# Layer 0 of a two-layer image block: TensorE's strip in eight runs of one tile shape, paired 64-column matmuls, two-bank PSUM buffers and a pinned VectorE order

## The chip, the cores and the metric

The kernel runs on one core of one Trainium2 chip. The metric is the device time in microseconds (us) of one execution; the time before is the median of three runs. One more execution was taken by the hardware profiler, and every row of the profile comes from that one.

## What is computed

`x` is (4, 64, 256, 256) in float32. Two layers run one after the other, each on a group-normalised input, and each adds its result to `x`. The change touches layer 0 alone:

```
x  = x + L0(group_norm(x))          # layer 0, changed
x  = x + L1(group_norm(x))          # layer 1, two state-space blocks and a fusion, unchanged

L0: h = w_in x                      # 64 -> 3*170 channels
    gate, x_sp, x_fr = split(h)
    sp = depthwise 3x3 conv(x_sp)
    fr = irfft2(rfft2(x_fr in 8x8 patches) * fft_weight)
    out = w_out (gelu(gate) * (sp + fr))   # 170 -> 64 channels
```

## The kernel before

Layer 0 cuts each of the four images (batches) into 32 strips of 8 rows, so 128 strips in all. The 170 channels are worked on as 64 + 64 channels ("a") and 42 channels ("b"), which take different ways.

For the 128 "a" channels the 3x3 convolution is done on TensorE. `products` (L726) forms it from sums and differences of neighbouring input columns: `v14` (difference, by GpSimd, L657) and `v23` (sum and difference, by VectorE, L659 and L660), into two PSUM tiles `m14` and `m23`, in a "third" part whose contraction is 64 rows deep (tile shape 64\*128) and a full part (128\*128). A strip has two halves of its columns, so each of these comes twice. ScalarE copies a part of `m23` out (L748) and VectorE makes the two outer combinations `y` from it (L750, L751).

For the spectral branch, `spec1` (L676) transposes patches and multiplies by `w_in` (64\*128, three groups of tiles per strip, copied out by ScalarE into `hs`, L689), `spec2` (L691) transforms (64\*64, three groups, scaled out by VectorE into `hw`, L702). `inverse_a` (L753) adds the inverse transform of the "a" channels onto `m14` (64 columns wide, shape 128\*64), and `inverse_b` (L778) does that for the 42 "b" channels into a PSUM tile `fr` (shape 128\*42).

The "b" channels' convolution is nine multiply-adds on VectorE (`tap_b`, L797 to L806) on `xat` and its row-swapped copy `xen`, made by `inputs_b` (L707, with a DMA at L724) one strip ahead. `gate_a` and `gate_b` (L767, L790) make the gates, ScalarE applies the Gelu, VectorE multiplies. `project` (L812) makes the output for a half strip, VectorE adds the residual (L827) and takes statistics for layer 1 (L830), and a DMA writes the strip to `x1d` (L836).

In one turn of the strip loop three strips are in work: `cur`, the one ahead of it (`nxt`, whose inputs are loaded and transformed) and the one behind it (`prev`, which is gated and projected). TensorE runs in exactly the written order: `mm` (L195) keeps every matmul in program order, so the list of calls at the end of the loop is its order. VectorE, ScalarE, GpSimd and SP (which issues all DMAs) are put in order by the scheduler. The input statistics of the next batch (`stat_add`, L167 to L169, two VectorE instructions a strip) are written at the head of the turn and are free to move; they wait for the loads of `sx` (L161). At the last strip of a batch the next batch's normalisation is worked out from them (`group_norm`, L135 to L152), and the first `spec1` of that batch needs it.

[...] `m14` and `m23` take two each, `fr` one, `po` (projection) one, and all other uses (`spec1`, `spec2`, both gates, `inputs_b`) share a single two-bank buffer named "two". Of the tiles in SBUF, `at` and `er` have three buffers, `pr`, `pn`, `xat`, `xen`, `v14`, `v23` two, `hs`, `acc`, `fub`, `geb` one.

Of the kernel before, what the change touches and what calls it, by code (L numbers as in the profile page):

```python
# [16 lines left out]
C = 64  # L17
# [91 lines left out]
def tile_kernel(ctx: ExitStack, tc: tile.TileContext, x, cst, w0, winp, wdwp, w1, out):  # L109
# [74 lines left out]
    with ExitStack() as l0:  # L184
# [433 lines left out]
        pp = l0.enter_context(tc.tile_pool(name="ps0", bufs=1, space=PSUM))  # L618
        wk = l0.enter_context(tc.tile_pool(name="wk0", bufs=2))

        fr = new(pp, [P, 4, 128], "fr")
        nc.vector.memset(fr, 0.0)
# [3 lines left out]
        def load(b, s, nm, rs):  # L626
# [25 lines left out]
            if s == NS0 - 1:  # L652
# [6 lines left out]
            nc.vector.tensor_tensor(v23[:, :, 0], d1, d2, ALU.add)  # L659
            nc.vector.tensor_tensor(v23[:, :, 1], d2, d1, ALU.subtract)  # L660
# [6 lines left out]
                "v14": v14.rearrange("p r (c k) -> p r k c", k=2), "v23": v23,  # L667
                "hs": new(wk, [P, 2, 4, 2, HID], "hs", 1), "hw": new(wk, [P, 2, 8, HID], "hw"),
            }

# [20 lines left out]
        def spec2(t, i):  # L691
            u0, u1 = UNITS[i]
            n = (u1 - u0) * HID
            ps = new(pp, [P, 2, 512], "two")
            for k in range(2):
                for w in range(2):
                    p = slice(w * C, (w + 1) * C)
                    mm(
                        ps[k * C : (k + 1) * C, w, :n], lhsT=con("qf")[p],
                        rhs=t["hs"][p, k].rearrange("p a h c -> p (a h c)")[:, u0 * HID : u1 * HID], start=True, stop=True,  # L700
                    )
            nc.vector.tensor_tensor(  # L702
                t["hw"][:, :, u0:u1], ps[:, :, :n].rearrange("p w (u c) -> p w u c", c=HID),
                wsp.unsqueeze(1).unsqueeze(1).to_broadcast([P, 2, u1 - u0, HID]), ALU.mult,
            )

        def inputs_b(t):  # L707

            b, s = t["b"], t["s"]
            if s == 0:  # L710
                ps = new(pp, [P, 2, 512], "two").rearrange("p q (r c) -> p (q r) c", c=S)
                mm(ps[:, 0], lhsT=xb, rhs=t["at"][:, 0, 1 : S + 1], start=True, stop=True)
                nc.scalar.copy(t["xat"][:, 0, 1 : S + 1], ps[:, 0])
            else:
                nc.scalar.copy(t["xat"][:, 0], last_at[b][:, 4])
            ps = new(pp, [P, 2, 512], "two").rearrange("p q (r c) -> p (q r) c", c=S)
            for i in range(2):
                mm(
                    ps[:, 2 * i : 2 * i + 2], lhsT=xb, rhs=t["at"][:, 1 + 2 * i : 3 + 2 * i, 1 : S + 1], start=True, stop=True
                )  # L720
            nc.scalar.copy(t["xat"][:, 1:5, 1 : S + 1], ps)
            last_at[b] = t["xat"]
            for k in range(2):
                nc.sync.dma_start(out=t["xen"][k * C : (k + 1) * C], in_=t["xat"][(1 - k) * C : (2 - k) * C, k : k + 4])  # L724

        def products(t, half, name, third):  # L726
# [3 lines left out]
            if third:  # L730
                t[name] = new(pp, [P, 2, 2, 4, 64], name)
# [14 lines left out]
            ps = t.pop("m23").rearrange("p e k m c -> p e k (m c)")  # L746
            m3 = new(wk, [P, 2, 256], "m3")
            nc.scalar.copy(m3, ps[:, :, 1])  # L748
            t["y"] = new(wk, [P, 2, 2, 256], "y", 2)
            nc.vector.tensor_tensor(t["y"][:, :, 0], ps[:, :, 0], m3, ALU.add)  # L750
            nc.vector.tensor_tensor(t["y"][:, :, 1], ps[:, :, 0], m3, ALU.subtract)  # L751

        def inverse_a(t, half):  # L753
            ps = t.pop("m14")
            for j in range(8):
                for e in range(2):
                    for g in range(2):
                        c = slice(g * C, (g + 1) * C)
                        mm(
                            ps[c, e, :, :, j * 8 : (j + 1) * 8], lhsT=t["hw"][:, j // 4, 2 * (j % 4) + half, c],  # L760
                            rhs=con("qj")[:, e * C : (e + 1) * C].rearrange("p (k m c) -> p k m c", k=2, m=4),
                            start=False, stop=(j == 7),
                        )
            y = t["y", half] = t.pop("y").rearrange("p e k x -> p (e k x)")
            nc.vector.tensor_tensor(y, ps.rearrange("p e k m c -> p (e k m c)"), y, ALU.add)  # L765

        def gate_a(t, half):  # L767
# [5 lines left out]
            ge, fu = new(wk, [P, 1024], "ge"), new(wk, [P, 2, 512], "fu", 3)  # L773
            nc.scalar.activation(ge, pg.rearrange("p e x -> p (e x)"), AF.Gelu)
            nc.vector.tensor_tensor(fu.rearrange("p e x -> p (e x)"), t.pop(("y", half)), ge, ALU.mult)
            t["fu", half] = fu

        def inverse_b(t, half):  # L778
            n = HID - 128
            for j in range(8):  # L780
                for o in range(2):
                    mm(
                        fr[o * C : o * C + n, :, j * 16 : (j + 1) * 16], lhsT=t["hw"][:, j // 4, 2 * (j % 4) + half, 128:HID],
                        rhs=con("qi2")[:, o * C : (o + 1) * C].rearrange("p (m c) -> p m c", m=4),
                        start=True, stop=True,
                    )
            o = t["acc"][:, :, half * 128 : (half + 1) * 128]
            nc.vector.tensor_tensor(o, fr, o, ALU.add)

        def gate_b(t):  # L790
            ps = new(pp, [P, 2, 512], "two").rearrange("p q (r c) -> p (q r) c", c=S)
            for i in range(2):
                mm(ps[:, 2 * i : 2 * i + 2], lhsT=gw[:, 2, :], rhs=t["en"][:, 2 * i : 2 * i + 2, :], start=True, stop=True)
            t["geb"] = new(wk, [P, 4, S], "geb", 1)
            nc.scalar.activation(t["geb"], ps, AF.Gelu)

        def tap_b(t, k):  # L797
            dy, dx = k // 3, k % 3
            src = (t["xat"][:, 0:4], t["xen"], t["xat"][:, 1:5])[dy]
            if k == 0:  # L800
                t["acc"] = new(wk, [P, 4, S], "acc", 1)
                nc.vector.tensor_scalar(t["acc"], src[:, :, dx : dx + S], taps[:, 0:1], None, ALU.mult)
                return
            nc.vector.scalar_tensor_tensor(  # L804
# [3 lines left out]
        def fuse_b(t):  # L808
            t["fub"] = new(wk, [P, 4, S], "fub", 1)
            nc.vector.tensor_tensor(t["fub"], t["acc"], t["geb"], ALU.mult)  # L810

        def project(t, half):  # L812
            po = new(pp, [P, 2, 4, 64], "po")
            h = slice(half * 64, (half + 1) * 64)

            def split(v):
                return v.rearrange("p m (c k) -> p k m c", k=2)[:, :, :, h]

            mm(po, lhsT=ow[:, 2, :], rhs=split(t["fub"]), start=True, stop=False)
            fu = t.pop(("fu", half))  # L820
            for e in range(2):
                mm(
                    po[e * C : (e + 1) * C].rearrange("p k m c -> p (k m c)"), lhsT=oa, rhs=fu[:, e], start=False, stop=True
                )
            if half == 0:
                t["x1"] = new(wk, [P, 4, S], "x1")
            nc.vector.tensor_tensor(split(t["x1"]), po, split(t["er"]), ALU.add)  # L827
            c0 = half * 128
            o = t["x1"][:, :, c0 : c0 + 128]
            nc.vector.bn_stats(t["stats2"][:, 2 * t["s"] + half, :], o)  # L830
            if half == 1:
                if t["s"] == NS0 - 1:
                    moments(moments2[t["b"]], t["stats2"])
                r0 = t["s"] * R0
                for k in range(2):
                    nc.sync.dma_start(  # L836
                        out=x1d[t["b"]][:, r0 + k : r0 + R0 : 2, :], in_=t["x1"][k * C : (k + 1) * C]
                    )
# [11 lines left out]
        inputs_b(cur)  # L850
        prev = None
        nxt_stats = None
        for b in range(nb):
            for s in range(NS0):
                if b + 1 < nb:
                    if s == 0:
                        nxt_stats = new(wk, [P, 2 * NS0, 6], "stats1")
                    stat_add(stat_load(ld, b + 1, s), s, nxt_stats)
                if s + 1 < NS0:
                    nxt = load(b, s + 1, *norm)  # L860
                elif b + 1 < nb:
                    norm = norm_of(nxt_stats)
                    nxt = load(b + 1, 0, *norm)
                else:
                    nxt = None

# [8 lines left out]
                def filter_b(*ks):  # L875
                    for k in ks:
                        tap_b(cur, k)

                products(cur, 0, "m23", True)
                behind(gate_a, 1)  # L880
                filter_b(0)
                products(cur, 0, "m23", False)
                ahead(spec1, 0)
                products(cur, 0, "m14", True)
                filter_b(1)
                products(cur, 0, "m14", False)
                ahead(spec1, 1)
                filter_b(2)
                inverse_a(cur, 0)
                inverse_b(cur, 0)  # L890
                ahead(spec2, 0)
                behind(project, 0)
                filter_b(3)
                ahead(inputs_b)
                products(cur, 1, "m23", True)
                products(cur, 1, "m23", False)
                gate_a(cur, 0)
                products(cur, 1, "m14", True)
                filter_b(4)
                ahead(spec2, 1)  # L900
                products(cur, 1, "m14", False)
                filter_b(5)
                gate_b(cur)
                inverse_a(cur, 1)
                filter_b(6)
                ahead(spec1, 2)
                inverse_b(cur, 1)
                ahead(spec2, 2)
                filter_b(7)
                behind(project, 1)  # L910
                filter_b(8)
# [3 lines left out]
        for half in range(2):  # L915
            project(prev, half)
# [575 lines left out]
```

## Time and profile before

| what | value |
|---|---|
| median of three runs (9519.37 to 9529.17) | 9528.11 us |
| the profiled execution, its own time | 9531.23 us |
| its span, first to last instruction | 9529.5 us |
| mean granted TensorE clock | 0.984 |
| layer 0's strips: first TensorE record to last write of x1d issued | 168 to 4696 us |
| a strip, start to start (median of all) | 34.20 us |
| the three strips at the edge between two batches | 43.6, 44.2 and 43.6 us |
| the last strip | 27.4 us |

A start of a strip is taken here where its `gate_b` starts on TensorE, which happens once a strip. The page gives each engine's busy time, and its rows name an instruction by line, engine, operation and tiles (out<-in). For TensorE a row gives the tile shape first (64\*128: 64 rows by 128 columns of the array) and then the sizes. PE is the matmul stream, PEld the weight loads, which can run beside it; L197 is the helper `mm`, so for TensorE one goes by the tiles' names. Since matmuls are pipelined, a record's duration reaches over the start of the next one: the pace is read from start to start. On VectorE, too, an instruction starts some 0.08 us before the one ahead of it ends, unless it needs its result. Idle time is given with what ended it; "issue" means that the profile shows no wait.

### The profile page before, as it was taken

Reading aid. Unit: us, or ns where it says so; the run is one execution under the profiler, and the core shown is the slowest. Engines: PE = TensorE matmul, PEld = TensorE weight load, DVE = VectorE, ACT = ScalarE, POOL = GpSimd, SP = SyncE. Lnnn points to the kernel's source line nnn. Section 1 sums busy time; section 2 is a strip of 40 time slices with the busy share of each in tenths; the row PEclk is TensorE's granted clock in tenths of the full one; section 3 lists DMA queues with packets and bytes.
Section 4 is the critical chain, followed back from the end, with each engine's and each line's share of the span. In section 5 each row is a group of like instructions: output and inputs, shape, how many; then the busy total and the mean of one; then the engine's idle time right before and its main releaser. Section 6 shows DMA issues by size and latency. Waiting matters only on the chain. (4 is left out here: it accounts for less than half of the span.)

```text
span 9529.5 us, 179824 instructions
## 1 busy us (share of the span) xinstructions
PE 9001.7 (94%) x76918; PEld 5698.1 (60%) x76918; DVE 7028.1 (74%) x8960; ACT 2803.2 (29%) x4570; POOL 3348.5 (35%) x2177
## 2 busy tenths in 40 slices
PE   3889999999999999999999999999999999999999
PEld 2555555555555555555565666656666566665666
DVE  6888777777777778777667776777667767667676
ACT  2222222222222222222362222622226222272222
POOL 4111122111121122111265444654436544375443
PEclk9999999999999999999999999999999999999999
DMA  7664333333333333333361333613336233362332
GB/s 172 151 151 103 82 78 82 82 82 81 81 81 81 81 79 84 81 81 81 87 203 50 79 89 91 192 64 89 85 84 194 74 85 83 84 195 74 84 81 71
DMA packets 655565, 938.21 MB, mean 98 GB/s; under 512 B 43184, under 2 KB 584880, under 8 KB 619184
## 3 DMA queue, kind: packets, MB, share of 16 engines
q1 hardware_dynamic: 654768, 926.71, 37.6%
q8 instruction: 606, 9.93, 0.4%
q14 instruction: 191, 1.56, 0.1%
HBM read 583.86 MB, written 275.05 MB: 90 GB/s over the span
## 5 line engine op out<-in xcount | busy, mean ns | idle before, releaser
L197 PE MATMUL m<-v,sw 64*128 64x256 f32 (+1 forms) x8192 | 1601.1, 398 | 0.0
L197 PEld LDWEIGHTS m<-v,sw 64*128 64x128 f32 (+1 forms) x8192 | 1106.4, 189 | 701.2 <-issue 570.8
L1307 POOL TENSOR_TENSOR xr<-xr,fx 128x512 f32<-128x512 f32 x512 | 651.5, 1272 | 1860.7 <-ACT xr L1306 1370.3
L1204 PE MATMUL pst<-fx,wb 64*128 64x256 f32 (+1 forms) x4992 | 1015.8, 437 | 37.4 <-DVE stm L1210 18.3
L765 DVE TENSOR_TENSOR y<-m,y 128x1024 f32<-128x1024 f32 x256 | 313.0, 1223 | 704.5 <-PE m L197 704.5
L804 DVE SCALAR_TENSOR_TENSOR acc<-xat,taps,acc 128x1024 f32<-128x1024 f32 x640 | 819.5, 1281 | 8.2
L1337 POOL TENSOR_TENSOR rs<-ve,mhalf 128x32 f32<-128x32 f32 x128 | 695.5, 5433 | 99.3 <-DVE ve L1210 99.3
L1204 PEld LDWEIGHTS pst<-fx,wb 64*128 64x128 f32 (+1 forms) x4992 | 508.1, 186 | 370.9 <-issue 244.3
L646 POOL MEMSET at<- 128x10 f32 x128 | 14.4, 113 | 1970.6 <-DMA at<-in_x_dram 1700.1
L1210 DVE SCALAR_TENSOR_TENSOR stm<-stm,step,pst 128x512 f32<-128x512 f32 x640 | 478.5, 748 | 232.8 <-PE pst L1204 219.3
L1308 ACT ACTIVATE sq<-xr 128x512 f32<-128x512 f32 x512 | 322.8, 630 | 875.3 <-POOL xr L1307 875.3
L1204 PE MATMUL px<-wb,xr 128*128 128x128 f32 x4096 | 575.0, 284 | 0.0
L197 PEld LDWEIGHTS m<-ct,hw 128*64 128x64 f32 x16384 | 498.5, 138 | 122.0 <-issue 122.0
L1210 DVE SCALAR_TENSOR_TENSOR sto<-sto,step,pst 128x512 f32<-128x512 f32 x512 | 382.8, 748 | 242.5 <-PE pst L1204 231.3
L1204 PEld LDWEIGHTS px<-wb,xr 128*128 128x128 f32 x4096 | 524.9, 194 | 54.2 <-issue 41.8
L689 ACT COPY hs<-two 128x1020 f32<-128x1020 f32 (+1 forms) x384 | 352.1, 917 | 692.6 <-PE two L197 692.6
L197 PE MATMUL m<-ct,hw 128*64 128x64 f32 x16384 | 533.9, 224 | 0.0
L1204 PE MATMUL ph<-sto,wb 128*64 128x128 f32 (+1 forms) x5120 | 528.0, 299 | 0.0
L1204 PE MATMUL ph<-stm,wb 128*64 128x128 f32 (+1 forms) x5120 | 525.0, 299 | 0.0
L1210 DVE TENSOR_TENSOR y<-px,rs 128x512 f32<-128x512 f32 x512 | 354.0, 691 | 231.7 <-PE px L1204 222.7
L1204 PEld LDWEIGHTS ph<-stm,wb 128*64 128x64 f32 (+1 forms) x5120 | 408.9, 147 | 144.6 <-issue 128.1
L804 DVE SCALAR_TENSOR_TENSOR acc<-xen,taps,acc 128x1024 f32<-128x1024 f32 x384 | 492.2, 1282 | 4.2
(319 smaller groups left out, 16636.8 us busy)
## 6 DMA issues: line engine op xcount, KB each, us to landing
strip<-x1d SPq DMA_DIRECT2D x512, 256.0 KB, 7.3
fx<-fxd SPq DMA_DIRECT2D x128, 1024.0 KB, 6.9
at<-in_x_dram SPq DMA_DIRECT2D x248, 320.0 KB, 5.5
xen<-xat SPq DMA_DIRECT2D x256, 258.0 KB, 4.8
sx<-in_x_dram SPq DMA_DIRECT2D x256, 256.0 KB, 4.6
pr<-in_x_dram SPq DMA_DIRECT2D x256, 256.0 KB, 4.1
er<-in_x_dram SPq DMA_DIRECT2D x256, 256.0 KB, 4.7
x1d<-x SPq DMA_DIRECT2D x256, 256.0 KB, 3.4
```

What stands on the lines that cost most here:

```text
L197: tc.keep_in_program_order(nc.tensor.matmul(*args, **kw))
L646: nc.gpsimd.memset(at[:, :, 0 : S + 2 : S + 1], 0.0)
L689: nc.scalar.copy(hs.rearrange("p k h c -> p h k c"), ps[:, :, : n * HID].rearrange("p h (k c) -> p h k c", k=n))
L765: nc.vector.tensor_tensor(y, ps.rearrange("p e k m c -> p (e k m c)"), y, ALU.add)
L804: nc.vector.scalar_tensor_tensor(t["acc"], src[:, :, dx : dx + S], taps[:, k : k + 1], t["acc"], ALU.mult, ALU.add)
L1204: tc.keep_in_program_order(nc.tensor.matmul(*args, **kw))
L1210: return lambda *args, **kw: tc.keep_in_program_order(getattr(nc.vector, name)(*args, **kw))
L1307: nc.gpsimd.tensor_tensor(xr, xr, fx, ALU.add)
L1308: nc.scalar.activation(sq, xr, AF.Square)
L1337: nc.gpsimd.tensor_tensor(r, ve.rearrange("p n c -> p (n c)"), mhalf, ALU.pow)
```

## The change

The same work is put in another order, in other PSUM buffers.

- TensorE's list is written anew so that calls of one tile shape stand together: the third parts of `m23` and `m14` with two `spec1` and `gate_a`; the full parts; `inverse_b` for the whole strip with `project` for the whole strip and `inverse_a`; two `spec2`; and the same for the second half with `gate_b`, `inputs_b` and the last `spec2`.
- `inputs_b`, `gate_b` and the "b" part of `project`, which were matmuls with 128-column weights, become pairs with 64-column weights.
- `inverse_b` takes 64 columns of `hw` in place of 42; `hw` is now one of two fixed tiles with 32 spare columns.
- `fr` and `po` lose their own PSUM banks; "two" has two buffers of two banks, and `fr` and `po` are taken from it.
- Every VectorE instruction of layer 0's strips keeps its program order (`InOrder`). `products`, `inverse_a`, `gate_a` and `project` are cut so that their VectorE parts (`middle`, `outer`, `fuse_a`, `add_b`, `residual`, `finish`) have places of their own; `sums_in` (the two `v23` instructions) moves to the end of the turn before; the input statistics are given two places in the turn (`count`).

```diff
-        pp = l0.enter_context(tc.tile_pool(name="ps0", bufs=1, space=PSUM))
+        pp = l0.enter_context(tc.tile_pool(name="ps0", bufs=2, space=PSUM))
...
-        fr = new(pp, [P, 4, 128], "fr")
-        nc.vector.memset(fr, 0.0)
+        class InOrder:
+            def __getattr__(self, name):
+                return lambda *args, **kw: tc.keep_in_program_order(getattr(nc.vector, name)(*args, **kw))
+        vec = InOrder()
+        hws = [new(wk, [P, 2 * 8 * HID + 32], f"hw{k}", 1) for k in range(2)]
...
+        def sums_in(t, k):
+            d1, d2 = t["d"]
+            vec.tensor_tensor(t["v23"][:, :, k], d2, d1, ALU.subtract if k else ALU.add)
...
             for i in range(2):
-                mm(ps[:, 2 * i : 2 * i + 2], lhsT=gw[:, 2, :], rhs=t["en"][:, 2 * i : 2 * i + 2, :], start=True, stop=True)
+                for h in range(2):
+                    p = slice(h * C, (h + 1) * C)
+                    mm(
+                        ps[p, 2 * i : 2 * i + 2], lhsT=gw[:, 2, p], rhs=t["en"][:, 2 * i : 2 * i + 2, :], start=True, stop=True
+                    )
...
-                t[name] = new(pp, [P, 2, 2, 4, 64], name)
+                t[name] = new(pp, [P, 2, 2, 4, 64], name, 1)
...
+        def inverse_b(t):
+            ps = t["fr"] = new(pp, [P, 2, 512], "two")
+            for half in range(2):
+                v = ps[:, half].rearrange("p (m c) -> p m c", m=4)
+                for j in range(8):
+                    for o in range(2):
+                        mm(
+                            v[o * C : (o + 1) * C, :, j * 16 : (j + 1) * 16], lhsT=spectral(t, half, j, 128),
...
+        def add_b(t):
+            o = t["acc"].rearrange("p m (f c) -> p f m c", f=2)
+            vec.tensor_tensor(o, t.pop("fr").rearrange("p f (m c) -> p f m c", m=4), o, ALU.add)
...
+        def project(t):
+            po = t["po"] = new(pp, [P, 2, 512], "two")
+            for half in range(2):
+                fu = t.pop(("fu", half))
+                for e in range(2):
+                    p = slice(e * C, (e + 1) * C)
+                    mm(
+                        po[p, half].rearrange("p (k m c) -> p k m c", k=2, m=4), lhsT=ow[:, 2, p], rhs=split(t["fub"], half),
+                        start=True, stop=False,
                     )
+                for e in range(2):
+                    mm(po[e * C : (e + 1) * C, half], lhsT=oa, rhs=fu[:, e], start=False, stop=True)
...
                 products(cur, 0, "m23", True)
-                behind(gate_a, 1)
-                filter_b(0)
-                products(cur, 0, "m23", False)
                 ahead(spec1, 0)
                 products(cur, 0, "m14", True)
-                filter_b(1)
+                ahead(spec1, 1)
+                behind(gate_a, 1)
+                tap_b(cur, 0)
+                tap_b(cur, 1)
+                count(0)
+                behind(fuse_a, 1)
+                products(cur, 0, "m23", False)
+                middle(cur)
                 products(cur, 0, "m14", False)
-                ahead(spec1, 1)
-                filter_b(2)
+                tap_b(cur, 2)
+                inverse_b(cur)
+                add_b(cur)
+                tap_b(cur, 3)
+                behind(project)
+                behind(residual)
+                count(1)
                 inverse_a(cur, 0)
-                inverse_b(cur, 0)
+                outer(cur, 0)
                 ahead(spec2, 0)
-                behind(project, 0)
-                filter_b(3)
-                ahead(inputs_b)
+                ahead(spec2, 1)
                 products(cur, 1, "m23", True)
-                products(cur, 1, "m23", False)
                 gate_a(cur, 0)
                 products(cur, 1, "m14", True)
-                filter_b(4)
-                ahead(spec2, 1)
+                ahead(spec1, 2)
+                behind(finish)
+                fuse_a(cur, 0)
+                tap_b(cur, 4)
+                products(cur, 1, "m23", False)
+                middle(cur)
                 products(cur, 1, "m14", False)
-                filter_b(5)
+                tap_b(cur, 5)
+                inverse_a(cur, 1)
+                outer(cur, 1)
                 gate_b(cur)
-                inverse_a(cur, 1)
-                filter_b(6)
-                ahead(spec1, 2)
-                inverse_b(cur, 1)
+                ahead(inputs_b)
+                tap_b(cur, 6)
+                ahead(sums_in, 0)
+                tap_b(cur, 7)
+                ahead(sums_in, 1)
+                tap_b(cur, 8)
                 ahead(spec2, 2)
-                filter_b(7)
-                behind(project, 1)
-                filter_b(8)
                 fuse_b(cur)
                 prev, cur = cur, nxt
```

## The prediction

> **What bounds the kernel now.** I read the page first, then TensorE's instructions in order of time over one strip of layer 0, then the stretches of layer 0 against each other, then VectorE and GpSimd where they meet. The page's busy shares name TensorE:
>
> ```profile
> PE 9001.7 (94%) x76918; PEld 5698.1 (60%) x76918; DVE 7028.1 (74%) x8960; ACT 2803.2 (29%) x4570; POOL 3348.5 (35%) x2177
> ```
>
> But 94% busy is not 94% streaming. TensorE in order of time (start us, duration us; each fp32 matmul leaves two records):
>
> ```profile
> 3005.45 0.80 PE L197 MATMUL two<-hs,ct 64*64 64x340 f32 x8
> 3006.18 1.17 PE L197 MATMUL po<-fub,w0t 128*128 128x512 f32 x2
> 3007.28 1.08 PE L197 MATMUL po<-fu,oa 128*64 128x512 f32 x4
> 3008.29 1.14 PE L197 MATMUL m<-v,sw 64*128 64x256 f32 x8
> ...
> 3010.25 1.99 PE L197 MATMUL m<-v,sw 128*128 128x256 f32 x8
> 3012.18 1.14 PE L197 MATMUL two<-w0t,pn 64*128 64x170 f32 x12
> 3013.15 3.08 PE L197 MATMUL m<-v,sw 64*128 64x256 f32 x16
> 3016.15 1.14 PE L197 MATMUL two<-w0t,pn 64*128 64x170 f32 x12
> 3017.22 2.09 PE L197 MATMUL m<-ct,hw 128*64 128x64 f32 x64
> 3019.14 1.06 PE L197 MATMUL fr<-ct,hw 128*42 128x64 f32 x32
> 3020.13 1.09 PE L197 MATMUL two<-hs,ct 64*64 64x510 f32 x8
> ...
> 3022.24 1.08 PE L197 MATMUL po<-fu,oa 128*64 128x512 f32 x4
> 3023.68 1.99 PE L197 MATMUL two<-at,xb 128*128 128x512 f32 x4 [0.36 <-DVE hw L702]
> 3025.60 3.06 PE L197 MATMUL m<-v,sw 64*128 64x256 f32 x16
> ```
>
> and its weight loads over the run that starts at 3023.68:
>
> ```profile
> 3024.22 0.19 PEld L197 LDWEIGHTS two<-at,xb 128*128 128x128 f32 x1 [0.24 <-issue]
> 3024.65 0.19 PEld L197 LDWEIGHTS two<-at,xb 128*128 128x128 f32 x1 [0.24 <-issue]
> ```
>
> A 512-column pass takes 0.43 us (3024.22 to 3024.65). Four are 1.72, yet the next run starts 1.92 after the first: 0.20 is spent where the tile shape (the 128*128 or 64*128 ahead of the sizes) changes. The same x12 group takes 0.97 when the shape stays (3012.18 to 3013.15) and 1.07 when it changes after it (3016.15 to 3017.22)[...]. With 64-column weights two pairs of passes take 1.01 (3007.28 to 3008.29) for 0.86: 0.15. From 128*64 to 128*42 nothing is lost (64 records in 1.92), so that is one shape. A strip of 34.20 us (median start to start) has 21 such runs.
>
> Layer 0's strips are not all alike. Fourteen early ones and fourteen later ones (us, PE, DVE, ACT, POOL busy, clock, DMA share, GB/s):
>
> ```profile
> 221.12:791.21 570.09, 499.02 (x4755) 293.72 (x4753) 488.19 (x587) 116.36 (x140) 101.89 (x101) 0.94 0.62 150
> 825.40:1304.30 478.90, 470.76 (x4762) 283.41 (x4761) 380.19 (x406) 117.89 (x140) 93.71 (x101) 1.00 0.35 82
> ```
>
> The early ones take 40.7 us, with 181 more VectorE instructions:
>
> ```profile
> L169 DVE BATCH_NORM_STATS2 stats<-sx x256: 665/682/735, 27.3 to 795.3; 128x6 f32<-128x512 f32 x128
> ```
>
> All 192 input statistics of batches 1 to 3 were pulled into these strips (the last runs at 795.3), and VectorE and the one "two" buffer hold TensorE back there.
>
> **The change, part by part (us for one strip).**
> Switches. Counted in the built order, runs fall from 21 to 8. Into shapes with 128-column weights there were 13 and are 4, with 64-column weights 8 and 4: 9 x 0.20 + 4 x 0.15 = 2.40 saved, all on TensorE, which is the path.
>
> Buffers. With one "two", TensorE stood for VectorE's hw (the 1.44 from 3022.24 to 3023.68 for 1.01) and ScalarE's ge. Over the strips from 800 to 4400 the runs ahead of spec2(1), inputs_b and gate_b exceed their stream and switch by 0.29, 0.44 and 0.21: 0.94. In the new order each "two" tile waits for the reader of the tile two back. Walking the strip with the durations of the rows I find each reader done in time, so these 0.94 go.
>
> Pairs. inputs_b, gate_b and project turn 12 full passes into 12 pairs of 64 columns. The near row is po<-fu: its pairs step by 0.43, like a full pass, so I take nothing. [...] The row at 3024.22 loads the same rows amid a pass, with no loss[...]. 64 columns in place of 42: 64 records cost 1.87 in m<-ct,hw (0.15 off the 2.02 of a lone run), two fr groups 2 x 0.88: +0.10.
>
> VectorE. The order is pinned with the same work plus two input statistics, and add_b in one instruction. By start-to-start times (tap 1.20, 1024-wide add 1.14, 512-wide 0.60) it is 28.1 busy per strip: under TensorE, but now everything queued behind a waiting instruction waits too. In the walk most such waits (for inverse_b, project, m23) are repaid in VectorE's slack. One isn't: the next strip's second m23 pair needs sums_in(1), pinned behind outer(1), tap 6, sums_in(0), tap 7. From inverse_a(1)'s end that chain is 0.2 + 1.14 + 1.20 + 0.74 + 1.20 + 0.96 + 0.06 = 5.5. TensorE has gate_b 1.73, inputs_b 1.73, spec2(2) 0.57, two switches and the first m23 pair, 4.8. So a new wait of 0.7[...]: 0.8. tap 8, hw and fub behind it are not late for project, 10 us on.
>
> GpSimd. A tap behind a GpSimd instruction:
>
> ```profile
> 1366.82 1.42 POOL L156 TENSOR_SCALAR at<-at,nm,rs 128x1280 f32<-128x1280 f32 x1
> 1367.67 1.63 DVE L804 SCALAR_TENSOR_TENSOR acc<-xen,taps,acc 128x1024 f32<-128x1024 f32 x1
> ```
>
> 1.63 for 1.28. The 2.32 us v14 subtraction meets only adds out of PSUM (still 1.22) and statistics before, never a tap. [...] v14 is released by m14's last pass, exactly where tap 5 starts. By the row for adds v14 costs nothing[...]. From m23's last pass tap 5 is 0.42 + 0.59 + 0.03 + 1.20 = 2.24 away (ACT's wait, its copy, two VectorE instructions), v14 1.79 + 0.48 = 2.27. I take tap 5 first, 0.25. The other GpSimd steps fall beside PSUM work.
>
> SP and ACT. SP now takes xen, at, x1d, er, sx, pr in turn; at is issued four strips ahead, behind sums_in, and lands in 5.5. xen, issued at the strip's end, lands some 6 us on, ahead of tap 3 at 12. ACT's row copy waits for tap 8 and GpSimd's memset; hs behind it ends 0.2 before gate_a needs it. Nothing for these.
>
> Sum: 34.20 - 2.40 - 0.94 + 0.10 + 0.80 + 0.25 = 32.0.
>
> Early strips. The statistics are pinned at two a strip and have room, so these 14 come to 32.0 as well. Batch edges: three strips take 43.8 now, 9.6 over. The new statistics start only when fub is through; then aggregation 1.88, two small matmuls, four small steps, GpSimd's power 0.57 and two normalisations 1.53 before spec1: I get 12.1 over, 44.1. The last strip loses some 2.
>
> Whole: 109 x 2.2 + 14 x 8.7 - 3 x 0.3 + 2 = 363. Layer 1 (from 4697 on) is untouched. From the profiled execution's own 9531.2 that gives 9168; it lies 3 over the median of the runs, so 9165.
>
> **Rivals.**
> GpSimd first. If v14 takes the port 0.03 us sooner than I work out, tap 5 starts 2.1 late, and outer(1) and sums_in with it: 33.0 a strip, 123 more, 9288. For it: the margin is a few hundredths. Against: both follow one TensorE stream, so the order is the same every strip.
> No port trouble. v14 and the taps pass, or v14 ends sooner: 31.75, -31, 9134[...]. For it: no row shows v14 against a tap.
> Slower: pairs that don't run side by side. Both pairs of inputs_b and gate_b read the same rows; if each then took its own pass, 12 x 0.43 = 5.2 more, of which the 1.05 of waiting at the strip's edge is covered: 36.1, or 9670. It decides from a pair of 0.76 us (break-even 34.9 a strip). Against: inverse_a's pairs share their moving operand and step by 0.06 us, the pace of one.
> That the change doesn't do what it says is out: the built order has the eight runs and the pinned VectorE.
>
> **How the numbers follow.** Forecast 9165: 0.48. GpSimd first, 9288: 0.24. No port trouble, 9134 or lower: 0.18. Slower, 9670: 0.05. Other waits that I don't see, strips of 33.5 and more but still faster: 0.05. The range 9105 to 9295 takes in the first three and leaves 0.1 to 0.15 out. Faster by over 0.2% (19 us, about what a measurement of this kernel can tell from no change) 0.94, within it 0.01, slower 0.05.
>
> **What would show it.** Eight runs a strip, each boundary still 0.20 or 0.15. The first 14 strips like the others. TensorE's wait in a strip almost all on sums_in (about 1 us at the strip's start), none on ge or hw. tap 6, not tap 5, at 1.5 us; if tap 5 shows over 3 us, the rival holds. inputs_b's four passes 1.73 apart from its switch. I am wrong if a second wait of over 0.3 us stands in TensorE's strip, or if a pair steps by more than 0.5.

## The result and the profile after

| | us |
|---|---|
| before, median of four runs beside it | 9526.48 |
| after, median of four runs (9403.77 to 9406.1) | 9405.12 |
| after / before, 95% interval | 0.9874 (0.9857 to 0.9891) |
| span of the profiled execution after | 9403.1 |

121 us were gained where 363 were forecast. TensorE's busy time fell by 202 us, VectorE's rose by 318 and GpSimd's by 303, though GpSimd's instructions are the same 2177: the first sign that the two hold each other up.

```profile
PE 8799.6 (94%) x78454; PEld 5836.8 (62%) x78454; DVE 7346.4 (78%) x8833; ACT 2785.1 (30%) x4570; POOL 3651.7 (39%) x2177
```

TensorE after, in order of time over the edge of a strip (start us, duration us, and in brackets the idle time ahead and what ended it):

```profile
2986.57 1.89 PE L197 MATMUL two<-at,xb 128*64 128x512 f32 x8
2988.39 0.80 PE L197 MATMUL two<-hs,ct 64*64 64x340 f32 x8
2989.70 0.70 PE L197 MATMUL m<-v,sw 64*128 64x256 f32 x4 [0.51 <-DVE v L625]
2991.63 1.22 PE L197 MATMUL m<-v,sw 64*128 64x256 f32 x4 [1.23 <-DVE v L625]
2992.64 1.91 PE L197 MATMUL two<-w0t,pn 64*128 64x170 f32 x12
2994.34 1.40 PE L197 MATMUL m<-v,sw 64*128 64x256 f32 x8
2995.58 1.03 PE L197 MATMUL two<-w0t,pn 64*128 64x170 f32 x12
2996.44 1.06 PE L197 MATMUL two<-en,ga 64*128 64x512 f32 x4
```

Two things are to be seen. TensorE waits twice for a sum that VectorE makes, 0.51 and 1.23 us. And behind the wait the same group of twelve passes takes 1.70 us (2992.64 to 2994.34), which takes 0.86 a little later (2995.58 to 2996.44). That is TensorE's clock, as the slices of 1 us show (stretch, length, PE, PEld, DVE, ACT, POOL busy, granted clock, DMA share, GB/s):

```profile
2991.00:2992.00 1.00, 0.37 (x2) 0.37 (x4) 1.00 (x2) 0.00 (x0) 0.00 (x0) 0.81 1.02 194
2992.00:2993.00 1.00, 1.00 (x8) 0.83 (x8) 1.00 (x2) 0.00 (x0) 0.11 (x1) 0.50 0.80 264
2993.00:2994.00 1.00, 1.00 (x10) 1.00 (x8) 1.00 (x2) 0.41 (x1) 0.00 (x0) 0.50 0.56 141
2994.00:2995.00 1.00, 1.00 (x8) 0.91 (x8) 0.86 (x2) 0.40 (x1) 0.00 (x0) 0.50 1.13 276
2995.00:2996.00 1.00, 1.00 (x12) 0.89 (x12) 0.96 (x2) 0.61 (x1) 0.00 (x0) 0.98 1.17 231
```

If the clock is either whole or half, twice the missing share is the time at half: 2 x (0.19 + 0.5 + 0.5 + 0.5 + 0.02) = 3.42 us. It doesn't happen in every strip. The first fourteen together, then three strips one by one (cut here where `inputs_b` starts, right behind `gate_b`):

```profile
238.36:717.44 479.08, 454.79 (x4930) 301.67 (x4928) 433.52 (x421) 115.99 (x141) 133.04 (x98) 0.96 0.41 97
2986.79:3021.46 34.67, 32.94 (x354) 21.96 (x352) 30.89 (x31) 8.31 (x10) 9.25 (x7) 0.95 0.40 96
3021.46:3054.49 33.03, 31.30 (x354) 20.51 (x352) 30.54 (x31) 8.21 (x10) 10.11 (x7) 1.00 0.45 101
3054.49:3089.17 34.68, 32.94 (x354) 21.95 (x352) 30.97 (x31) 8.31 (x10) 9.25 (x7) 0.95 0.40 96
```

Strips of 34.7, 34.7 and 33.0 us follow each other in turn nearly everywhere; 77 of 127 are long ones, and the mean is 34.1, so outside the first fourteen the strip gained 0.1 us. The long ones have a clock of 0.95. The first fourteen, 40.7 us each before, are now like the others (34.2).

Why TensorE waits is seen on VectorE:

```profile
3016.53 1.29 DVE L625 TENSOR_TENSOR y<-m,m 128x512 f32<-128x512 f32 x2 [0.53 <-ACT m L762]
3017.74 3.43 DVE L625 SCALAR_TENSOR_TENSOR acc<-xen,taps,acc 128x1024 f32<-128x1024 f32 x1
3021.09 1.21 DVE L625 TENSOR_TENSOR y<-m,y 128x1024 f32<-128x1024 f32 x1
3022.22 1.27 DVE L625 SCALAR_TENSOR_TENSOR acc<-xat,taps,acc 128x1024 f32<-128x1024 f32 x1
3023.42 0.91 DVE L625 TENSOR_TENSOR v<-at 128x640 f32<-128x640 f32 x1
```

and on GpSimd at the same time:

```profile
3017.76 2.32 POOL L666 TENSOR_TENSOR v<-at 128x1280 f32<-128x1280 f32 x1 [0.54 <-PE m L197]
```

Tap 5 takes 3.43 us for 1.28. It ends at 3021.17, 1.08 after v14 (3017.76 + 2.32 = 3020.08): it did its work behind v14. Everything behind it is late, the outer sum (3021.09) and the first sum for TensorE (3023.42) included. It is so in 118 of the 128 strips: tap 5 takes 3.38 to 3.43 us in them and ends 1.08 after v14 each time.

### The profile page after: what moved, and what is told of

Same layout as the page of the kernel before. It is cut to its first block, busy times and chain, and to the rows that moved or that the text cites. A ratio compares the mean times of both kernels' runs of the same rounds, so it can differ in the third digit from the quotient of the medians.

```text
span 9403.1 us, 182768 instructions
## 1 busy us (share of the span) xinstructions
PE 8799.6 (94%) x78454; PEld 5836.8 (62%) x78454; DVE 7346.4 (78%) x8833; ACT 2785.1 (30%) x4570; POOL 3651.7 (39%) x2177
## 5 line engine op out<-in xcount | busy, mean ns | idle before, releaser
L197 PE MATMUL m<-v,sw 64*128 64x256 f32 (+1 forms) x8192 | 1643.1, 414 | 209.6 <-DVE v L625 209.6
L197 PEld LDWEIGHTS m<-v,sw 64*128 64x128 f32 (+1 forms) x8192 | 1160.9, 200 | 769.7 <-DVE v L625 330.5
L156 POOL TENSOR_SCALAR pn<-pr,nm,rs 128x512 f32<-128x512 f32 x256 | 387.5, 1521 | 1411.4 <-PE two L197 1406.2
L625 DVE SCALAR_TENSOR_TENSOR acc<-xen,taps,acc 128x1024 f32<-128x1024 f32 x384 | 750.1, 1953 | 4.5
L797 ACT ACTIVATE ge<-two 128x1024 f32<-128x1024 f32 x256 | 262.8, 1026 | 1593.8 <-PE two L197 1593.7
L1096 POOL TENSOR_TENSOR sd<-fh 128x1024 f32<-128x1024 f32 x128 | 380.3, 2991 | 298.4 <-PE pv L1034 225.4
```

The costliest lines, as they stand in the source:

```text
L156: nc.gpsimd.tensor_scalar(o, i, nm, rs, ALU.add, ALU.mult)
L197: tc.keep_in_program_order(nc.tensor.matmul(*args, **kw))
L625: return lambda *args, **kw: tc.keep_in_program_order(getattr(nc.vector, name)(*args, **kw))
L797: nc.scalar.activation(t["ge"], pg.rearrange("p e x -> p (e x)"), AF.Gelu)
L1096: e.tensor_tensor(t, f[:, :n], f[:, : n - 1 : -1], op)
```

## The experiments

Theory P: v14 blocks tap 5, VectorE is 2.15 us late, TensorE waits at the strip's edge, and in most strips the wait also costs it half its clock for 3.4 us. "The port", in the prediction and in the expectations, is the author's name for what v14 and a tap can't have at the same time; the traces show the waiting alone (3.43 us for 1.28). Rivals are named with each run. Each ratio is to the kernel before.

**1. The two sums first.** In the strip loop:

```
-                tap_b(cur, 6)
                 ahead(sums_in, 0)
-                tap_b(cur, 7)
                 ahead(sums_in, 1)
+                tap_b(cur, 6)
+                tap_b(cur, 7)
                 tap_b(cur, 8)
```

> The changed kernel with one thing in VectorE's order altered: the two sums for the next strip stand ahead of taps 6, 7 and 8, no longer between them. In the changed kernel a strip is 34.7, 34.7, 33.0 us in turn (mean 34.1). Theory P (port and clock): GpSimd's v14 holds tap 5 (3.43 us), the chain from there to the sums makes TensorE wait 1.95 us at the strip's edge, and in two strips of three the wait also halves TensorE's clock for some 3.4 us (1.65 us lost). Tap 5 stays at 3.43 us here, but the sums come 1.2 and 2.4 us earlier, the wait falls to 0.3 us or less, the clock stays whole: strip 31.8 to 32.1, total 9115 to 9150. Rival R (the half clock has nothing to do with the wait): the wait goes, the clock still drops in two strips of three: strip 33.0, total 9265. Rival Q (VectorE as pinned is the bound, its taps only change places): strip unchanged at 34.1, total 9405.

Measured: 9406.36, ratio 0.9873 (0.9857 to 0.9890); strips of 34.7 and 33.1. None of the theories' mechanisms as put, though Q's number holds: the sums came early, and TensorE waited as long for the next thing, spec1(1)'s "two" buffer, which hw frees behind tap 8. TensorE after its two sums:

```profile
2993.06 1.07 PE L197 MATMUL m<-v,sw 64*128 64x256 f32 x8
2996.02 1.27 PE L197 MATMUL two<-w0t,pn 64*128 64x170 f32 x12 [1.89 <-DVE hw L625]
```

So it isn't the sums' place. VectorE as a whole is late, and of its results the one needed next shows the wait.

**2. v14 left out.** It is computed for the first two strips alone; all others read those two tiles, so this kernel's result is not the layer's.

```
+            if b == 0 and s < 2:
                 nc.gpsimd.tensor_tensor(v14, ...)
```

> The changed kernel without GpSimd's v14 after the first two strips: two tiles computed once are read by all strips (the other strips' v14 is left out, so m14 holds wrong values). VectorE's and TensorE's instructions are the same. Theory P: tap 5 is 1.28 us, the wait for the sums under 0.8 us, the clock whole: strip 31.7, as in the one strip near the end that has no v14 beside it (31.73); total 9095 to 9120. Rival Q (pinned order alone): the wait stays, strip 33 to 34, total 9265 to 9405.

Measured: 9111.69, ratio 0.9565 (0.9550 to 0.9579); every strip 31.63 but at the batch edges, the mean clock 0.987 for 0.973 in the changed kernel, and tap 5 at its own length:

```profile
1449.22 1.28 DVE L625 SCALAR_TENSOR_TENSOR acc<-xen,taps,acc 128x1024 f32<-128x1024 f32 x1
```

P holds, Q falls: the pinned order alone leaves a wait of 0.4.

**3. Passes of no use in the wait.** spec2(2)'s four passes are done twice, and between the two waits:

```
+  for i in range(10):   # 5 in the second run
+      mm(ps[:, i % 2, 0], lhsT=zz[q], rhs=v[q, ...], start=False, stop=False)   # zz is zero
```

> The changed kernel with passes added to TensorE in its wait at the strip's edge: the last spectral step's 4 passes are done twice and, between the waits for the first and the second sum, 10 passes with weights of zero are added into m23. The results are the same; VectorE's order and the port are untouched. Theory P: tap 5 stays at 3.43 us and the sums come as late as before, but TensorE is no longer idle for 1.95 us, so its clock stays whole in every strip: 33.0 to 33.2 in all of them instead of 34.7, 34.7, 33.0; total 9265 to 9295 (80 strips by 1.65 us less). Rival R (the clock drops for another reason): the cycle of three stays, total 9405 or, with the added passes at half clock, some 9420.

> The run with passes added in TensorE's wait, with 5 added zero-weight passes in place of 10. There every strip took 33.87 us, with a whole clock: the 10 passes, 0.216 us each, filled 2.16 us where the second wait is 1.23, and so put 0.84 us on top of 33.03. 5 take 1.08 and fit. Theory P2: 33.0 to 33.15 in all strips, total 9405 - 77 strips by 1.65 us = 9278, at most 9295. Rival R (the clock drops for another reason than the wait, and the longer filler only shifted it): strips of 34.7 come back, total 9350 to 9405.

Measured: 9388.62, ratio 0.9856 (0.9842 to 0.9871), with ten; 9304.64, ratio 0.9770 (0.9754 to 0.9786), with five. Ten overfilled the wait: every strip but those at the batch edges was 33.87 us, with a clock of 1.00. With five, 119 of the strips are 33.2, and not one of 34.7 is left. The five passes (ten records), and a long stretch with them, whose clock is 1.00 (behind the busy times):

```profile
1450.10 1.46 PE L197 MATMUL m<-v,zz 64*128 64x256 f32 x10
```

```profile
800.00:4100.00 3300.00, 3265.44 (x36396) 2168.74 (x36396) 3027.31 (x2924) 807.04 (x982) 948.19 (x703) 1.00 0.40 96
```

Both totals are over what was expected, the first by the 0.84 us of overfilling, the second by the 0.18 us a strip that five passes still cost. That TensorE does more work and the kernel is 100 us shorter than the changed one settles it for this kernel: the half clock came of the wait, and rival R falls. Tap 5 stays at 3.43 in both.

**4. v14 at another time.** Its instruction is written behind `residual`, with a wait for it:

```
-  nc.gpsimd.tensor_tensor(v14, at[:, :, 0:S], at[:, :, 2 : S + 2], ALU.subtract)   # in load
...
   behind(residual)
+  ahead(outer_in, prev)      # the same tensor_tensor, waits for prev's second x1 sum
```

> The changed kernel with v14 at another time and nothing left out: GpSimd computes it when VectorE has written the residual (a wait for that instruction), beside outer, hw and hw, which read PSUM. VectorE's order is that of the changed kernel. Theory P2: tap 5 is 1.28 us, v14 2.3 us or less, TensorE waits 0.6 us at the strip's edge, and the clock stays whole: strip 31.6 to 31.8 as without v14 (31.63, 9111.7), total 9105 to 9140. Rival M (the port only moves: v14 lengthens the outer sum or hw beside it, or at and en lengthen fu and tap 2): strip 32.5 to 34, total 9210 to 9400.

Measured: 9113.12, ratio 0.9565 (0.9551 to 0.9579). v14 itself is as long as before, and so is all beside it. VectorE, then GpSimd:

```profile
1440.37 0.68 DVE L625 BATCH_NORM_STATS2 stats<-sx 128x6 f32<-128x512 f32 x1
1441.03 1.23 DVE L625 TENSOR_TENSOR y<-m,y 128x1024 f32<-128x1024 f32 x1
1442.17 2.54 DVE L625 TENSOR_TENSOR hw<-two,wsp 128x1020 f32<-128x1020 f32 x2
```

```profile
1440.54 2.32 POOL L679 TENSOR_TENSOR v<-at 128x1280 f32<-128x1280 f32 x1 [4.33 <-DVE x L625]
```

Nothing was left out, and the time is that of experiment 2: v14 cost nothing beside these instructions (0.68, 1.23 and 1.27 us each, v14 2.32), which have at most one input in SBUF, and 292 us in all on top of a tap (3.43 for 1.28), which has two. This version takes 4.4% off the kernel before and 3.1% off the changed one.

**5. v14 a tenth of a microsecond later.** As in 4, but tied to the second y sum ahead of tap 5, so that it comes close to where the changed kernel has it:

```
   middle(cur)
+  ahead(outer_in, cur)       # waits for cur's second y sum
```

> The changed kernel with v14 tied to the second of the two y sums ahead of tap 5 (it starts when that has ended) and no longer to TensorE's last m14 pass: some 0.1 us later than in the changed kernel. There tap 5's record begins at 3017.735, before v14's (3017.765), but it can't have the port before the y sum ahead of it ends (3017.817), and it takes 3.43 us. Theory P2 (who asks first keeps the port to its end): v14 now comes about 0.1 us after tap 5, tap 5 takes 1.28 us, v14 waits and is recorded at 3.3 to 3.6 us, tap 6 is blocked for 0.2 to 0.5 us; strip 31.8 to 32.2, total 9130 to 9185. Rival G (GpSimd wins the port whenever both want it): tap 5 stays at 3.4 us, strip 33.0 to 34.1, total 9265 to 9405.

Measured: 9125.20, ratio 0.9577 (0.9563 to 0.9591); strips of 31.73. VectorE and GpSimd, to be laid beside the rows at 3017.74 above:

```profile
1457.50 1.28 DVE L625 SCALAR_TENSOR_TENSOR acc<-xen,taps,acc 128x1024 f32<-128x1024 f32 x1
1459.51 1.23 DVE L625 TENSOR_TENSOR y<-m,y 128x1024 f32<-128x1024 f32 x1 [0.73 <-PE m L197]
1460.65 1.39 DVE L625 SCALAR_TENSOR_TENSOR acc<-xat,taps,acc 128x1024 f32<-128x1024 f32 x1
```

```profile
1457.67 3.29 POOL L679 TENSOR_TENSOR v<-at 128x1280 f32<-128x1280 f32 x1 [0.68 <-DVE y L625]
```

Now v14 is the one that waits (3.29 for 2.32) and tap 5 isn't touched; tap 6 pays 0.11. v14's record starts 0.17 us after tap 5's here, and started 0.03 after it in the changed kernel. That tenth is worth 280 us. Rival G (GpSimd always wins) falls. The trace of the changed kernel has the same contrast: in all 118 strips with a long tap 5, v14's record starts 0.05 to 0.10 us ahead of the end of VectorE's instruction before the tap (the second y sum); in the one strip where it starts 0.01 after that end, the tap takes 1.28 and v14 3.36.

**6. hw brought forward as well**, alone and together with 4:

```
+  ahead(sums_in, 0); ahead(sums_in, 1)
   tap_b(cur, 6)
+  ahead(spec2, 2)            # hw
   tap_b(cur, 7)
   tap_b(cur, 8)
```

> The changed kernel with VectorE's order altered further than in the run that moved the sums alone (there TensorE's wait only moved on to spec1(1)'s buffer, which hw frees behind the taps: 1.9 us, same time). Here both sums, tap 6 and hw stand ahead of taps 7 and 8. Theory P2 (v14 puts VectorE 2.15 us behind, and TensorE waits for whatever of VectorE's work stands last ahead of the strip's edge): tap 5 stays at 3.43 us, but only fub waits for taps 7 and 8, and TensorE needs fub 10 us later; the wait at the edge is under 0.7 us and the clock stays whole: strip 31.4 to 32.2, total 9065 to 9165. Rival Q (VectorE is full, whatever stands first): the wait turns up again, at gate_a's fu or at the residual, strip 33.0 to 34.1, total 9265 to 9405.

> Both: v14 beside the residual, and both sums, tap 6 and hw ahead of taps 7 and 8. Theory P2: with VectorE 2.15 us earlier and what TensorE waits for in front, TensorE's strip has no wait left but what switches and the last spectral step cost: 31.0 to 31.4, total 9035 to 9085. Rival Q: not under the run with v14 moved alone (31.6 and over).

Measured: 9545.22, ratio 1.0021 (1.0014 to 1.0029), alone; 9232.69, ratio 0.9691 (0.9677 to 0.9706), together. Both missed. Of the run alone, all engines in order of time:

```profile
1454.14 1.28 DVE L625 SCALAR_TENSOR_TENSOR acc<-xat,taps,acc 128x1024 f32<-128x1024 f32 x1
...
1455.54 0.11 POOL L671 MEMSET xat<- 128x10 f32 x1 [8.45 <-DVE acc L625]
1455.68 0.41 ACT L727 COPY xat<-xat 128x258 f32<-128x258 f32 x1 [4.48 <-POOL xat L671]
1455.99 1.91 ACT L701 COPY hs<-two 128x1020 f32<-128x1020 f32 x2
...
1457.05 1.17 PE L197 MATMUL two<-en,ga 64*128 64x512 f32 x4 [2.48 <-ACT hs L701]
```

Tap 8 is the last reader of the old xat; GpSimd's memset waits for it, ScalarE's row copy for the memset, and both hs copies are queued behind that on ScalarE. What is brought ahead of tap 8 makes those late. My expectation had named only fub as waiting for taps 7 and 8. The wait of 2.48 costs the clock too (strips of 36.8, 35.3, 33.7 us, a clock of 0.95 from 800 to 4100 us). Together with 4, the same wait for `hs` is 1.37 us, the clock is 0.99 over that stretch, as in experiment 4, and a strip takes 32.61 for 31.63.

**7. Sums as a pair behind tap 6**, on top of 4 (tap 6, sum, sum, tap 7, tap 8, hw):

> The run with v14 beside the residual (9113 us), and both sums together behind tap 6, ahead of taps 7 and 8; hw stays behind tap 8, which ends no later. TensorE's wait for the second sum (0.38 us a strip) goes: strip 31.2 to 31.4, total 9060 to 9090. If the wait only moves on to spec1(1)'s buffer or to the hs copies, as in the runs where more was brought forward: 31.6, total 9105 to 9120.

Measured: 9114.47, ratio 0.9565 (0.9550 to 0.9579): the wait of 0.38 for a sum became one of 0.41 for hw. No gain, as in the second case of what was expected.

**8. The pairs undone**, on top of 4: gate_b, inputs_b and the fub part of project with 128 columns again.

```
-  for e in range(2):
-      mm(po[p, half]..., lhsT=ow[:, 2, p], rhs=split(t["fub"], half), ...)
+  mm(po[:, half]..., lhsT=ow[:, 2, :], rhs=split(t["fub"], half), ...)
```

> The run with v14 beside the residual (strip 31.63 us, 9113 us) with the pairs undone: gate_b, inputs_b and the fub part of project have weights of 128 columns again, half as many passes of 0.43 us each. TensorE's strip has five more switches between tile shapes (one at en and at, four around the two fub passes). If a switch costs 0.15 to 0.20 us as the passes' distances in the traces say and a pair of 64-column passes lies side by side: 0.75 to 1.0 us a strip more, total 9205 to 9245. Rival W (the pairs are not wholly side by side and cost what they save): no change, 9100 to 9125. Rival C (switches cost nothing in a strip that waits anyway): no change.

Measured: 9198.44, ratio 0.9654 (0.9639 to 0.9668). TensorE around project, with pairs (experiment 4):

```profile
1465.13 2.08 PE L197 MATMUL two<-ct,hw 128*64 128x64 f32 x64
1467.05 1.07 PE L197 MATMUL two<-fub,w0t 128*64 128x512 f32 x4
...
1470.57 2.04 PE L197 MATMUL m<-ct,hw 128*64 128x64 f32 x64
```

and without:

```profile
1461.10 2.08 PE L197 MATMUL two<-ct,hw 128*64 128x64 f32 x64
1463.12 1.17 PE L197 MATMUL two<-fub,w0t 128*128 128x512 f32 x2
...
1467.23 2.04 PE L197 MATMUL m<-ct,hw 128*64 128x64 f32 x64
```

6.13 us (1461.10 to 1467.23) against 5.44 for the same sums: four switches at 0.17. The fifth, at en and at, costs 0.19. Of these 0.88 the strip shows 0.68 (32.31 against 31.63), since the wait for the sum shrinks from 0.38 to 0.18; so the total is 7 us under what was expected. Rivals W and C fall.

**9. The counts paced in the kernel before.** Nothing else of the change:

```
-  stat_add(stat_load(ld, b + 1, s), s, nxt_stats)
+  counted = stat_load(ld, b + 1, s)
...
   filter_b(0)
+  stat_add(counted, s, nxt_stats, <each waits for this strip's tap 0>)
```

> The kernel before the change with one thing added: the two counts of the next batch's statistics are tied to their strip (each waits for tap 0 of that strip, on VectorE itself), so VectorE can't run ahead with them in the first strips. In the kernel before, the first 14 strips take 40.7 us each, the others 34.2. Theory P2 (of the 121 us gained, some 92 are the early strips, won by spreading the counts, and 20 the head; the strip itself, with its runs and pairs, gained 0.1): the first 14 strips fall to 34.2 to 35, total 9425 to 9450, with the strip otherwise as before. Rival E (the early strips were slow because their loads were late, or because of the order of TensorE): they stay near 40, total 9510 to 9530.

Measured: 9447.31, ratio 0.9917 (0.9900 to 0.9934). The first fourteen strips:

```profile
217.68:696.50 478.82, 469.11 (x4770) 283.26 (x4772) 401.28 (x432) 118.11 (x141) 100.42 (x99) 1.00 0.40 95
```

34.2 each, with a clock of 1.00 for 0.94 before. A few lines in the old kernel bring 79 us of the change's 121.

**10. VectorE's order left to the scheduler**, the rest as changed: `vec = nc.vector`.

> The changed kernel with VectorE's order left to the scheduler; TensorE's order, pairs and PSUM buffers stay. The statistics' counts run ahead in the first strips again, all taps stand in a row, and the sums and hw come early or late as they fall. Theory P2: the early strips are slow again (38 us and over, 80 to 100 us in all lost); the later ones depend on whether v14 meets a tap: 33 to 35; total 9400 to 9560, no better than the kernel before by more than 1.3%. Rival T (the pinned order is what costs, TensorE's part alone would have brought the 32 us of the prediction): strip 32, total 9180 to 9260.

Measured: 9370.45, ratio 0.9835 (0.9818 to 0.9851), better than the changed kernel by 35 us and under the expected span. The first sixteen strips take 36.9 to 40.9, as put; the later ones 33.25, all alike. There the taps stand ahead of hw and TensorE waits for hw, with a clock of 1.00 (900 to 4100 us):

```profile
1444.93 1.17 PE L197 MATMUL two<-en,ga 64*128 64x512 f32 x4 [1.58 <-DVE hw L714]
```

So pinning wins the early strips and, as it was laid out, loses 0.9 us in each of the others. Rival T falls: freeing VectorE doesn't bring 32.

## Why the prediction missed

**Right.** Eight runs a strip, and the switches' price: 0.17 to 0.19 each measured in experiment 8, for 0.20 and 0.15 in the sum. The pairs: en and at take 0.43 a pass as put, and undoing them brings only the switches back. The "two" buffer's waits are gone. The early strips are like the others. Without the two costs below, a strip is 31.63 to 31.73 (experiments 4 and 5), for 32.0 forecast. 34.20 less 31.63 is 2.57; with the wait of 0.38 that is left and the 0.10 for the wider `inverse_b`, some 3.05 of TensorE's 3.34 us of savings came about, and were given back.

**The step that failed** is GpSimd's: "I take tap 5 first, 0.25." (The 0.25 was the author's estimate; experiment 5, where tap 5 was first, shows 0.11, at tap 6.) The prediction's own signs were met: tap 5 is over 3 us, and a second wait of over 0.3 us stands in TensorE's strip. The two starts were worked out as 2.24 and 2.27 us after m23's last pass, and the trace has them 0.03 apart in just that order (3017.735 and 3017.765). But the order of the records isn't the order in which the two did their work. A VectorE record starts some 0.08 before the instruction ahead ends, and tap 5 follows the second y sum, which ends at 3017.817. Counting tap 5's turn from that end fits both traces: v14 came 0.05 before it and ran first in the changed kernel, came 0.08 after it and waited in experiment 5 (the counts over the changed kernel's strips stand there). The prediction had a tap that ran late behind a GpSimd instruction (1367.67: it ends 1.06 after `at`, which ends at 1368.24), and it had the fact about records, and didn't put the two together. The rival "GpSimd first" named what would be seen (tap 5 over 3 us) and gave 33.0 a strip, which is what the short strips take, 33.03; its total of 9288 is still 117 under the measured one. Tap 5's part is 1.30 over experiment 5 in 118 strips, 153 us.

**The term that was missing** is the clock. No part of the sum and no rival let a wait cost more than itself. A wait of 0.51 + 1.23 us costs 1.65 more in 77 strips, 127 us; experiment 3 won 100 of it, and its five passes cost 0.18 in 119 strips, 21. The trace shows more of the clock's loss: of the 83 stretches at half clock in layer 0's strips, 78 last 3.41 us and the other five a multiple of it, and they all start on one grid of 3.41 us, within 0.002. Cut along that grid, a long strip and then the short one behind it:

```profile
2988.22:2991.63 3.41, 1.68 (x14) 0.51 (x12) 3.41 (x5) 1.02 (x1) 0.00 (x0) 1.00 0.29 59
2991.63:2995.04 3.41, 3.41 (x20) 3.14 (x22) 3.28 (x4) 0.85 (x2) 0.11 (x1) 0.50 0.85 221
3022.35:3025.76 3.41, 2.22 (x16) 0.51 (x12) 3.41 (x4) 1.15 (x2) 0.00 (x0) 1.00 0.15 33
3025.76:3029.18 3.41, 2.87 (x32) 2.68 (x34) 3.41 (x4) 1.32 (x2) 0.11 (x1) 1.00 0.88 213
```

In the long strip both pieces of the wait fall into one cell of the grid: TensorE is busy for 1.68 us of it, and the next cell runs at half. In the short strip a line of the grid cuts the same wait in two (2.22 and 2.87 us busy), and the clock stays whole. From 204 to 4557 us after, the cells at whole clock that were followed by half clock have TensorE busy for at most 1.70 us (81 cells), those followed by whole clock for at least 1.97 (1100); before, from 222 to 4678 us, at most 1.52 (16) and at least 1.56 (1261). Three strips' 102.38 us (2986.79 to 3089.17) are thirty cells, hence the cycle of three. The trace of before had the sign: its first strips idle and have a clock of 0.94.

153 + 127 is 280. Against it, a strip with tap 5 first is 0.27 better than forecast (33 us in 123 strips) and the first strip starts 20 sooner; the batch edges and the last strip are 6 worse. That makes 233 of the 240 us missed; 7 are not assigned.

**Smaller.** "TensorE's wait almost all on sums_in" held, at 1.74 us in two pieces for 0.8 (0.7 worked out from the chain; the other 0.1 was the author's estimate, which no run shows). The batch edges are 46.0, 44.8 and 46.0 for 44.1 forecast. The last strip is unchanged (27.4), 2 less forecast. The first strip starts 20 us sooner than before (200.6 for 221.1), which the prediction didn't have; all runs with TensorE's new order have most of it (201 to 205 us), the paced kernel only 5 (215.8). What brings it was not tried. The other GpSimd steps do meet taps and fu (at takes 2.23 for 1.41 in the short strips), but no run took them apart. A third buffer each for v14 and pn, another way to let v14 go early, doesn't fit: it needs 153.3 KB of a partition where 144.8 are left, so it has no time. The mean strip of 34.1 lies in what the prediction called other waits that it didn't see, at 0.05.

## What to carry to other kernels

When two engines hold each other up, as v14 and tap 5 did here (3.43 us for 1.28), don't decide a race of hundredths on paper: give the movable instruction a place beside work that it doesn't delay (here bn_stats at 0.68, the y sum at 1.23 and hw at 1.27 us, with at most one input in SBUF), by a wait on that work. Where the trace shows half clock behind TensorE's idling, price the two together (here 1.74 us of waiting in two pieces cost another 1.65 in 77 of 127 strips), and look at the granted clock by strip, since a mean of 0.97 hides a 5% loss in two strips of three. Bringing one result forward on a full engine only hands the wait to the next one in its queue; follow each instruction that is passed over to its last reader first.

## What the runs showed of the hardware

- How much idling cost the clock here: with waits of 1.37 us (the mean of 93) and 1.58 us in one piece it was 0.99 and 1.00 over the strips from 800 or 900 to 4100 us (the run of both in experiment 6, experiment 10); with 1.74 in two pieces (the changed kernel) it was 0.95 in 77 strips and 1.00 in the short ones, with 1.90 in one piece (experiment 1) 0.97 over 800 to 4100 us, and with 2.48 (experiment 6, alone) 0.95.
- The half clock came in stretches of 3.41 us (78 of 83 in the changed kernel's layer 0) on a fixed grid of 3.41 us. The busiest cell of that grid with half clock behind it has 1.70 us of TensorE busy after and 1.52 before; the idlest with whole clock behind it has 1.97 after and 1.56 before.
- Passes with zero weights, added to an open sum, kept the clock at 1.00 from 800 to 4100 us (experiment 3): TensorE did more and the kernel was 100 us shorter.
- v14 and tap 5 did not do their work at the same time. In the changed kernel v14 took 2.32 us and tap 5 3.43, ending 1.08 after it; in experiment 5 tap 5 took 1.28 and v14 3.29, ending 2.18 after it. In the changed kernel's 118 strips with a long tap 5, v14 came 0.05 to 0.10 us ahead of the end of VectorE's instruction before it (3017.817 in the rows above); where it came after that end, by 0.01 (one strip of that kernel) or 0.08 (experiment 5's rows), tap 5 kept its 1.28.
- VectorE's bn_stats, with one input, was not lengthened by a v14 beside it (0.68), nor was an add out of PSUM (1.23).
